# Small matmuls of a window scan: dt's weights zero-padded to 128 rows, B's transposes taken over all rows

## The chip, the cores and the metric

The kernel runs on one core of one Trainium2 chip. The metric is the time of one execution on the device in microseconds (us); the median of three executions is compared. The core has five engines that run side by side, each with its own order of instructions: TensorE (PE in the profile; PEld is its weight loads), VectorE (DVE), ScalarE (ACT), GpSimd (POOL) and SyncE (SP), which here only issues DMAs.

## The reference, cut to what matters

Layer 0 is a triangle attention over an image of 256 x 256 pixels with 128 channels; nothing in it is touched. Layer 1 is a window scan. After a depthwise convolution, windows of 8 x 8 pixels of the upper and the lower half of the image are put in a Hilbert order and merged to sequences of L = 128 tokens; two orders (rows first, columns first), each scanned forwards and backwards, make K = 4 scans with 256 channels and a state of 16.

```python
x_dbl = jnp.einsum('bkdl,kcd->bkcl', xs, x_proj_w)                # 8 + 16 + 16 rows per scan
dts, Bs, Cs = jnp.split(x_dbl, [DT_RANK, DT_RANK + D_STATE], axis=2)
dts = jnp.einsum('bkrl,kdr->bkdl', dts, dt_projs_w)                 # 8 rows -> 256 channels
dts = jax.nn.softplus(dts + dt_projs_b[None, :, :, None])
A = -jnp.exp(A_logs).reshape(K, D_INNER, D_STATE)
...
def step(h, inp):
    u, dt, Bl, Cl = inp
    dA = jnp.exp(dt[..., None] * A)
    h = h * dA + (dt * u)[..., None] * Bl[:, :, None, :]
    y = jnp.einsum('bkdn,bkn->bkd', h, Cl)
    return (h, y)
```

The results of the four scans are added, put back in image order, normalised, gated with silu(z) and projected to 128 channels.

## The kernel before, in words

*Bands, jobs, units.* Layer 1 is cut into 64 bands (8 rows by 64 columns in each image half). A band has 4 jobs: two groups of four sequences (`g`), each in two orders (`o`). A job has 32 units: 2 directions (`back`) x 4 quarters of the state (`q`) x 2 channel halves (`dh`) x 2 pairs of sequences (`p`). All is float32, for which a matmul that is no transpose shows as two MATMUL instructions in the trace.

*One unit.* ACT makes the decay exp(dt A) (`decay`, tile `da`, L1172). TensorE spreads dt u B over state and tokens (`input`, `b_p<-diag,dut`, L1185): the stationary operand is dt u with the tokens on 64 partitions, the moving one a block-diagonal copy of B (`diag`), loaded from DRAM. Matmuls on partitions 0 to 63 and 64 to 127 take turns. DVE scans (`scan`, `h<-da,b_p`, L1205). GpSimd multiplies a pair of units with C (`weigh`, `h<-h,cc`, L1212). TensorE adds the four states up while it transposes (`reduce`, `y_p<-ident,h`, L1223). `b_p` has two buffers, so the input of unit i waits for the scan of unit i - 2.

*One job's preparation.* `u_mm` gathers the tokens in scan order, `xd_mm` projects them (L949): all 128 rows of `wx`, of which rows 0 to 7 are dt's forward rank, 32 to 39 the backward one, 64 to 95 B and 96 to 127 C, the rest zero. `xd_ev` adds 1 to rows 8 and 40, so that the dt bias can be a weight row. Then come the two steps that are changed:
- `bt_mm` (L961) writes C to DRAM and transposes B's 32 rows of `xd`, four blocks of 128 tokens, to `bt_p`; `bt_ev` copies that to `bt`, and `spread` writes it to the block diagonals in DRAM, from which `diag_load` reads.
- `dt_mm` (L1015) multiplies 9 rows of `xd` (8 of the rank, one of ones) with the 9 rows of `wdt` at partition 0 or 32, by direction; it is called 4 times per job. `dt_act` and `dt_max` make softplus of it on ACT and DVE, `du_mul` dt u on GpSimd, `dut_mm` and `dut_ev` the transposed dt u.

*Order of the work.* Layer 1's order is written out by hand. The main loop runs over the units; `own_script` (for the job to come) and `script` (for the running one) say at which unit each preparation step is issued, with its cost in columns on TensorE. What belongs to the neighbouring bands is filler: `conv` (`cv_p`), `expand` (`in_p`), `finish` (`z_p`, `w_p`, `gated`), `store` (`o_p`, `res`). Filler with a cost is issued at odd units when there is credit for it: every unit adds `rate`, every scripted step takes its cost off.

```python
    rate, cap, slack = 350, 800, 128
...
            credit = min(credit + rate, cap)
            for cost, call in calls:
                credit -= cost
                call()
```

So a scripted step's cost decides when the filler behind it is issued. In the text, slot n of TensorE is what stands between the inputs of unit n and of unit n + 1.

*Memory.* `wts` holds weights and constants: `wdt` one tile of 2 x 256 columns, `perm` the two orders and `permt` their transposes. PSUM is full: 4 banks of `b_p`, 2 of `y_p`, one for the scripted steps (`side`: `u_p`, `xd_p`, `bt_p`, `dt_p`, `dut_p`), one for the filler (`fill`).

Of the kernel before, what the change touches and what calls it, by code (L numbers as in the profile page):

```python
# [12 lines left out]
F32 = mybir.dt.float32  # L13
# [6 lines left out]
P = 128  # L20
# [5 lines left out]
DI = 256  # L26
NS = 16
DTR = 8
# [8 lines left out]
NBLK = 4  # L37
# [30 lines left out]
def kernel(  # L68
# [28 lines left out]
    nc = tc.nc  # L97
# [88 lines left out]
                    in_=x_proj[dh * P : (dh + 1) * P, k, lo : lo + n],  # L186
                )

    wdt = wts.tile([P, 2, DI], F32, name="wdt")
    for back in range(2):  # L190
        at = 32 * back
        nc.scalar.dma_start(
            out=wdt[at : at + DTR], in_=dt_w[:, 2 * back : 2 * back + 2]
        )
        for o in range(2):
            for dh in range(2):
                j = 2 * (o + 2 * back) + dh
                nc.scalar.dma_start(
                    out=wdt[at + DTR : at + DTR + 1, o, dh * P : (dh + 1) * P],
                    in_=dt_b[:, j : j + 1].rearrange("p j -> j p"),  # L200
                )
    units_at = wts.tile([P, 1], F32, name="units_at")
# [13 lines left out]


    perm = wts.tile([P, 2, P], F32, name="perm")
    permt = wts.tile([P, 2, P], F32, name="permt")
    halves_of = ident.rearrange("p (y f x) -> p y f x", y=WIN, f=2)  # L220
    for o, positions in enumerate(hilbert_positions()):
        for s, (wy, wx_) in enumerate(positions):
# [1 line left out]
                perm[:, o, 2 * s : 2 * s + 2], halves_of[:, wy, :, wx_]  # L224
            )
    with tc.tile_pool(name="pmp", bufs=1, space=PSUM) as pp:
        pt_p = pp.tile([P, 2, P], F32, name="pt_p")
        for o in range(2):
            nc.tensor.transpose(pt_p[:, o], perm[:, o], ident)
        nc.vector.tensor_copy(permt, pt_p)  # L230

        ca_p = pp.tile([P, P], F32, name="ca_p")
        nc.tensor.matmul(ca_p, perm[:, 0], perm[:, 1], start=True, stop=True)
        carry = wts.tile([P, P], F32, name="carry")
        nc.vector.tensor_copy(carry, ca_p)
# [432 lines left out]
    class Band:  # L668
# [125 lines left out]
        def finish(self, g):  # L794

            if self.gated is None:
                self.gated = one_p.tile([P, 2, NSEQ, SEQ], F32, name="gated")
            for s2 in range(GS // 2):
                s = g * GS + 2 * s2
                yield 512  # L800
                z_p = fill("z_p")
                for dh in range(2):
                    nc.tensor.matmul(
                        z_p[:, dh * DI : (dh + 1) * DI],
                        win[:, DI + dh * P : DI + (dh + 1) * P],
                        self.xg[:, 1 : 1 + WIN, :, 1 + s * WIN : 1 + (s + 2) * WIN]
                        .rearrange("p y f x -> p (y f) x")
                        .rearrange("p y (s x) -> p s y x", s=2),
                        start=True,
                        stop=True,  # L810
                    )
                yield -2

                ysum = self.ysb[g, 1][:, 2 * s2 : 2 * s2 + 2]
                e = two_p.tile([P, 512], F32, name="e")
                nc.vector.tensor_scalar(e, z_p, FLOOR, None, ALU.max)
                st = two_p.tile([P, 2, 6], F32, name="st")
                mv = two_p.tile([P, 2, 2], F32, name="mv")
                for j in range(2):
                    nc.vector.bn_stats(st[:, j], ysum[:, j])  # L820
                for j in range(2):
                    nc.vector.bn_aggr(mv[:, j], st[:, j])
                yield 0
                logistic(e)
                rs = two_p.tile([P, 2], F32, name="rs")
                rsqrt(rs, mv[:, :, 1])
                neg = two_p.tile([P, 2], F32, name="neg")
                nc.scalar.activation(neg, rs, AF.Copy, scale=-1.0)
                nb = two_p.tile([P, 2], F32, name="nb")
                for j in range(2):  # L830
                    nc.scalar.activation(
                        nb[:, j : j + 1],
                        mv[:, j, 0:1],
                        AF.Identity,
                        scale=neg[:, j : j + 1],
                    )
                yield -2
                nc.vector.tensor_mul(e, e, z_p)
                yn = one_p.tile([P, 2, DI], F32, name="yn")
                for j in range(2):  # L840
                    nc.scalar.activation(
                        yn[:, j],
                        ysum[:, j],
                        AF.Identity,
                        bias=nb[:, j : j + 1],
                        scale=rs[:, j : j + 1],
                    )
                yield 256
                w_p = fill("w_p")
                for dh in range(2):  # L850
                    for j in range(2):
                        nc.tensor.transpose(
                            w_p[:, dh * DI + j * P : dh * DI + (j + 1) * P],
                            yn[:, j, dh * P : (dh + 1) * P],
                            permt[:, 1],
                        )
                yield 0
                for dh in range(2):
                    half = w_p[:, dh * DI : (dh + 1) * DI]
                    nc.scalar.activation(  # L860
                        half,
                        half,
                        AF.Identity,
                        bias=lb1[:, dh : dh + 1],
                        scale=lw1[:, dh : dh + 1],
                    )
                yield -2
                nc.vector.tensor_mul(
                    self.gated[:, :, s : s + 2].rearrange("p d s l -> p d (s l)"),
                    w_p.rearrange("p (d l) -> p d l", d=2),  # L870
                    e.rearrange("p (d l) -> p d l", d=2),
                )
# [26 lines left out]
    def token_blocks(t):  # L899

        return t.rearrange("c (h s t) -> c h s t", h=2, s=GS)
# [5 lines left out]
    class Job:  # L907
# [53 lines left out]
        def bt_mm(self):  # L961
            self.c_d = cdr.tile([2 * NS, GT], F32, name="c_d")
            for h in range(2):
                nc.sync.dma_start(
                    out=token_order(self.c_d)[:, h],
                    in_=token_blocks(self.xd[96:128])[:, h],
                )
            self.bt_p = side("bt_p")
            for i in range(NBLK):
                nc.tensor.transpose(  # L970
                    self.bt_p[:, i * 32 : (i + 1) * 32],
                    self.xd[64:96, i * P : (i + 1) * P],
                    ident[64:96, 64:96],
                )

        def bt_ev(self):
            self.bt = two_p.tile([P, NBLK, 2, NS], F32, name="bt")
            nc.scalar.copy(
                self.bt.rearrange("p b k n -> p (b k n)"), self.bt_p[:, 0 : NBLK * 32]
            )  # L980

        def spread(self):
# [31 lines left out]

        def dt_mm(self, back, dh):  # L1015
            self.dt_p = side("dt_p")
            rows = slice(32 * back, 32 * back + DTR + 1)
            nc.tensor.matmul(  # L1018
                token_order(self.dt_p),
                wdt[rows, self.o, dh * P : (dh + 1) * P],  # L1020
                token_blocks(self.xd[rows]),
                start=True,
                stop=True,
            )
# [93 lines left out]
        def own_script(self):  # L1118

            return {  # L1120
                7: [(256, lambda: self.u_mm(0))],
                8: [(0, lambda: self.u_ev(0))],
                9: [(256, lambda: self.u_mm(1))],
                10: [(0, lambda: self.u_ev(1))],
                15: [(512, lambda: self.xd_mm(0))],
                16: [(512, lambda: self.xd_mm(1))],
                17: [(0, lambda: self.xd_ev())],
                18: [(128, lambda: self.bt_mm())],
                19: [(0, lambda: self.bt_ev())],
                20: [(512, lambda: self.dt_mm(0, 0)), (0, lambda: self.spread())],  # L1130
                21: [(0, lambda: self.dt_act(0, 0))],
                22: [(0, lambda: self.dt_max(0, 0))],
                23: [(512, lambda: self.dt_mm(0, 1))],
                24: [(0, lambda: self.dt_act(0, 1)), (0, lambda: self.diag_load(0, 0))],
                26: [(0, lambda: self.dt_max(0, 1))],
                28: [(256, lambda: self.dut_mm(0, 0))],
                29: [(0, lambda: self.dut_ev(0, 0))],
                30: [(256, lambda: self.dut_mm(0, 1))],
                31: [(0, lambda: self.dut_ev(0, 1))],
            }  # L1140
# [301 lines left out]
```

## Time and profile before

| | us |
|---|---|
| median of three executions | 23599.31 |
| their range | 23597.42 to 23599.98 |
| the profiled execution | 23598.3 |
| its span, first to last instruction | 23596.4 |

| engine | busy us | share of the span |
|---|---|---|
| TensorE, matmuls | 22824.2 | 97% |
| TensorE, weight loads | 16986.3 | 72% |
| VectorE | 21652.4 | 92% |
| GpSimd | 21292.1 | 90% |
| ScalarE | 18542.0 | 79% |

Layer 0 takes about the first 2420 us, layer 1 the rest. In layer 1 every band after the first shows the same period, 330.2 us from its first scan to that of the next, so one band stands for all. A line of the profile names the engine, the source line, the tile written and those read. Matmuls are pipelined: [...] what a matmul costs is read from one start to the next. An engine's idle time is put down to what ended it.

### The profile page before, as it was taken

How to read it: one execution, taken by the hardware profiler on the slowest of the kernel's cores; microseconds unless marked ns; L12 is line 12 of the kernel's file. 1: busy time of each engine (PE TensorE's matmuls, PEld its weight loads, DVE VectorE, ACT ScalarE, POOL GpSimd, SP SyncE). 2: the span in 40 equal slices, each digit the busy share in tenths (PEclk: the TensorE clock that was granted, in tenths of full speed). 3: DMA queues.
4: the chain of work that ended last, by engine and by line, in shares of the span. 5: the costliest groups of instructions: out<-in, count | busy, mean ns of one | idle time of the engine just before them, and what ended most of it. 6: DMA issues, size and time to landing. Idle time of an engine off the chain costs nothing.

```text
span 23596.4 us, 427303 instructions
## 1 busy us (share of the span) xinstructions
PE 22824.2 (97%) x171020; PEld 16986.3 (72%) x171020; DVE 21652.4 (92%) x17940; ACT 18542.0 (79%) x35206; POOL 21292.1 (90%) x5966
## 2 busy tenths in 40 slices
PE   7999999999999999999999999999999999999999
PEld 2555677777777777777777777777777777777777
DVE  6888899999999999999999999999999999999998
ACT  5999777777777777777777777777777777777777
POOL 3777899999999999999999999999999999999999
PEclk9999999999999999999999999999999999999999
DMA  5222444444444444444444444444444444444444
GB/s 200 76 74 72 146 160 159 161 162 160 161 158 162 161 160 159 160 163 160 161 159 160 162 160 162 158 161 162 160 159 161 162 161 160 158 161 162 160 160 147
DMA packets 2000327, 3638.76 MB, mean 154 GB/s; under 512 B 1129584, under 2 KB 1131760, under 8 KB 1725824
## 3 DMA queue, kind: packets, MB, share of 16 engines
q1 hardware_dynamic: 1985616, 3602.35, 45.7%
q8 instruction: 1347, 22.07, 0.4%
q10 hardware_dynamic: 12720, 9.07, 0.1%
q14 instruction: 644, 5.28, 0.1%
HBM read 3467.33 MB, written 143.65 MB: 153 GB/s over the span
## 4 chain that ended last, share of the span: by engine, by line
PE 67%; DVE 16%; ACT 9%; issue 8%; DMA 0%; ACTq 0%; POOLq 0%; SPq 0%; POOL 0%; DVEq 0%
PE b_p L1185 23%; PE y_p L1223 21%; DVE h L1205 14%; PE dt_p L1018 4%; PE cv_p L769 4%; PE xd_p L949 2%; ACT da L1172 2%; PE aT_p L522 1%; PE dut_p L1052 1%; PE sc L465 1%; ACT w_p L860 1%; PE in_p L721 1%; PE o_p L885 1%; ACT e L132 1%; PE v_p L383 1%
## 5 line engine op out<-in xcount | busy, mean ns | idle before, releaser
L1212 POOL TENSOR_TENSOR h<-h,cc 128x2048 f32<-128x2048 f32 x4096 | 18598.0, 4551 | 1318.2 <-POOL h L1212 560.7
L1205 DVE TENSOR_TENSOR_SCAN h<-da,b_p 128x1024 f32<-128x1024 f32 x8192 | 18245.8, 2271 | 1212.6 <-PE b_p L1185 1193.2
L1172 ACT ACTIVATE da<-dt,am 128x508 f32<-128x508 f32 x16384 | 10396.5, 707 | 853.3 <-DVE h L1205 853.2
L1185 PE MATMUL b_p<-diag,dut 64*128 64x256 f32 x65536 | 8561.4, 395 | 430.0 <-DVE h L1205 365.7
L1223 PEld LDWEIGHTS y_p<-ident,h 128*128 128x128 f32 x65536 | 7130.2, 140 | 1408.4 <-issue 1296.3
L1223 PE MATMUL y_p<-ident,h 128*128 128x128 f32 x65536 | 8008.8, 276 | 25.1 <-issue 19.4
L1185 PEld LDWEIGHTS b_p<-diag,dut 64*128 64x128 f32 x65536 | 5851.7, 186 | 2916.9 <-issue 1331.2
L738 ACT ACTIVATE tap<-xin,wtap 128x512 f32<-128x512 f32 x2048 | 1504.2, 744 | 349.1 <-PE cv_p L769 349.0
L1041 POOL TENSOR_TENSOR du<-dt,u 128x512 f32<-128x512 f32 x1024 | 1309.1, 1278 | 57.9 <-DVE dt L1034 57.9
L769 PE MATMUL cv_p<-ident,tap 128*128 128x128 f32 x9216 | 1273.7, 275 | 5.1 <-DVE xct L788 3.8
L769 PEld LDWEIGHTS cv_p<-ident,tap 128*128 128x128 f32 x9216 | 1047.4, 141 | 232.4 <-issue 228.2
L1028 ACT ACTIVATE sp<-dt_p 128x512 f32<-128x512 f32 x1024 | 603.1, 589 | 777.5 <-PE dt_p L1018 777.5
L452 POOL TENSOR_TENSOR tm<-trib,mb 128x2048 f32<-128x2048 f32 x256 | 1167.1, 4559 | 10.7
L1018 PE MATMUL dt_p<-xd,wdt 9*128 9x512 f32 x2048 | 1149.8, 641 | 2.5 <-DVE dt L1034 2.2
L493 ACT ACTIVATE at<-at,nmax 128x256 f32<-128x256 f32 x2048 | 1019.5, 502 | 0.0
L1061 ACT COPY dut<-dut_p 128x512 f32<-128x512 f32 x1024 | 583.8, 570 | 292.9 <-PE dut_p L1052 292.9
L1163 ACT ACTIVATE da<-ident 128x16 f32<-128x16 f32 x1536 | 346.0, 225 | 549.2 <-DVE h L1205 547.4
L1029 ACT ACTIVATE sp<-sp,one 128x512 f32<-128x512 f32 x1024 | 743.1, 726 | 33.3
L729 ACT COPY xin<-in_p 128x440 f32<-128x440 f32 x384 | 201.7, 525 | 718.6 <-PE in_p L721 718.6
L478 DVE CUSTOM_DVE_ANT_0 at<-sc,tm 128x256 f32<-128x256 f32 x2048 | 738.1, 417 | 7.9 <-PE sc L465 7.4
L1034 DVE SCALAR_TENSOR_TENSOR dt<-sp,dt_p 128x512 f32<-128x512 f32 x1024 | 677.9, 662 | 13.9 <-ACT sp L1029 13.9
L1052 PE MATMUL dut_p<-ident,du 128*128 128x128 f32 x4096 | 650.2, 281 | 13.7 <-ACT dut L1061 8.7
(132 smaller groups left out, 15502.6 us busy)
## 6 DMA issues: line engine op xcount, KB each, us to landing
cc<-c_d SPq DMA_DIRECT2D x2048, 1024.0 KB
diag<-z SPq DMA_DIRECT2D x1024, 1024.0 KB
xt<-in_x_dram SPq DMA_DIRECT2D x16, 2048.0 KB
xt<-in_x_dram SPq DMA_DIRECT2D x32, 1024.0 KB
xn_d<-xn SPq DMA_DIRECT2D x32, 1024.0 KB
xn<-xn_d SPq DMA_DIRECT2D x128, 256.0 KB
mb<-in_mask_dram SPq DMA_DIRECT2D x128, 256.0 KB
xr<-in_x_dram SPq DMA_DIRECT2D x128, 256.0 KB
```

The source lines that it names most:

```text
L452: nc.gpsimd.tensor_add(self.tm, trib.rearrange("p h m n -> p (h m) n"), self.pair.mb[:, self.row].unsqueeze(1).to_broadcast([P, 2 * NH, IMG]),
L493: nc.scalar.activation(self.at[hp][:, j, :], self.at[hp][:, j, :], AF.Exp, bias=self.nmax[hp][:, j : j + 1], scale=-1.0, accum_out=self.de ...
L738: nc.scalar.activation(scaled.rearrange("p s (y x) -> p s y x", x=WIN), self.xin[:, dh] .rearrange("p y f x -> p (y f) x")[:, 2 * dy : 2 * ...
L769: nc.tensor.matmul(cv_p[:, s], now[:, s], ident, start=(tap == 0 and s == 0), stop=(tap == 8 and s == GS - 1), is_transpose=True, skip_gro ...
L1018: nc.tensor.matmul(token_order(self.dt_p), wdt[rows, self.o, dh * P : (dh + 1) * P], token_blocks(self.xd[rows]), start=True, stop=True,)
L1041: nc.gpsimd.tensor_mul(token_blocks(du), token_order(self.dt[back][dh]), token_blocks(self.u[:, dh]),)
L1052: nc.tensor.transpose(self.dut_p[:, h * DI + dh * P : h * DI + (dh + 1) * P], self.du[back][dh][:, (2 * h + p) * P : (2 * h + p + 1) * P], ...
L1172: nc.scalar.activation(da[:, :, j, lo:hi], dt[:, :, lo:hi], AF.Exp, scale=am[:, a0 : a0 + 1])
L1185: nc.tensor.matmul(b_p[:, s, :, h * 64 : (h + 1) * 64].rearrange("p n t -> p t n"), job.dut[self.back][rows, p, h, self.dh * P : (self.dh ...
L1205: nc.vector.tensor_tensor_scan(out=out_, data0=d0, data1=d1, initial=0.0, op0=ALU.mult, op1=ALU.add)
L1212: nc.gpsimd.tensor_mul(self.pair, self.pair, cc.rearrange("p n s t -> p s n t"))
L1223: nc.tensor.matmul(job.y_p[:, 2 * p + s, self.dh * P : (self.dh + 1) * P], self.h[:, s, j], ident, start=(first and s == 0 and j == 0), st ...
```

## The change

`wdt` gets a tile of 128 rows for each direction, filled with zeros before the 9 rows of weights and bias are loaded; `dt_mm` multiplies all 128 rows of `xd`. `bt_mm` transposes all 128 rows of `xd`, so `bt_p` has 4 x 128 columns instead of 4 x 32, and `bt_ev` picks columns 64 to 95 of each block. The cost entered for `bt_mm` goes from 128 to 256. `bt` has one buffer instead of two, and of `permt` only the half that is read is kept. The other costs in the scripts stay.

```diff
-    wdt = wts.tile([P, 2, DI], F32, name="wdt")
+    wdt = wts.tile([P, 2, 2, DI], F32, name="wdt")
+    nc.vector.memset(wdt, 0.0)
     for back in range(2):
         at = 32 * back
         nc.scalar.dma_start(
-            out=wdt[at : at + DTR], in_=dt_w[:, 2 * back : 2 * back + 2]
+            out=wdt[at : at + DTR, back], in_=dt_w[:, 2 * back : 2 * back + 2]
         )
...
-                    out=wdt[at + DTR : at + DTR + 1, o, dh * P : (dh + 1) * P],
+                    out=wdt[at + DTR : at + DTR + 1, back, o, dh * P : (dh + 1) * P],
...
-    permt = wts.tile([P, 2, P], F32, name="permt")
+    permt = wts.tile([P, P], F32, name="permt")
...
-        pt_p = pp.tile([P, 2, P], F32, name="pt_p")
-        for o in range(2):
-            nc.tensor.transpose(pt_p[:, o], perm[:, o], ident)
+        pt_p = pp.tile([P, P], F32, name="pt_p")
+        nc.tensor.transpose(pt_p, perm[:, 1], ident)
...
-                            permt[:, 1],
+                            permt,
...
                 nc.tensor.transpose(
-                    self.bt_p[:, i * 32 : (i + 1) * 32],
-                    self.xd[64:96, i * P : (i + 1) * P],
-                    ident[64:96, 64:96],
+                    self.bt_p[:, i * P : (i + 1) * P],
+                    self.xd[:, i * P : (i + 1) * P],
+                    ident,
                 )
...
-            self.bt = two_p.tile([P, NBLK, 2, NS], F32, name="bt")
+            self.bt = two_p.tile([P, NBLK, 2, NS], F32, name="bt", bufs=1)
             nc.scalar.copy(
-                self.bt.rearrange("p b k n -> p (b k n)"), self.bt_p[:, 0 : NBLK * 32]
+                self.bt.rearrange("p b k n -> p b (k n)"),
+                self.bt_p.rearrange("p (b r) -> p b r", b=NBLK)[:, :, 64:96],
             )
...
-            rows = slice(32 * back, 32 * back + DTR + 1)
             nc.tensor.matmul(
                 token_order(self.dt_p),
-                wdt[rows, self.o, dh * P : (dh + 1) * P],
-                token_blocks(self.xd[rows]),
+                wdt[:, back, self.o, dh * P : (dh + 1) * P],
+                token_blocks(self.xd),
                 start=True,
                 stop=True,
             )
...
-                18: [(128, lambda: self.bt_mm())],
+                18: [(256, lambda: self.bt_mm())],
```

## The prediction

> **What bounds the kernel now.** I read the chain of the page first, then the stage table, the table of waits, and TensorE's timeline over one band.
>
> ```profile
> PE 67%; DVE 16%; ACT 9%; issue 8%; DMA 0%; ACTq 0%; POOLq 0%; SPq 0%; POOL 0%; DVEq 0%
> PE b_p L1185 23%; PE y_p L1223 21%; DVE h L1205 14%; PE dt_p L1018 4%; PE cv_p L769 4%; PE xd_p L949 2%; ACT da L1172 2%; PE aT_p L522 1%; PE dut_p L1052 1%; PE sc L465 1%; ACT w_p L860 1%; PE in_p L721 1%; PE o_p L885 1%; ACT e L132 1%; PE v_p L383 1%
> ```
>
> TensorE holds two thirds of the chain, and dt_p alone 4% of it, nearly all that it takes in total (1024 calls at 1.05 us or more are 4.6% of the span): most dt matmuls stand where TensorE decides. But the stage table, here for about one band of layer 1, shows three engines close together (busy: PE, PEld, DVE, ACT, POOL):
>
> ```profile
> 12000.00:12330.00 330.00, 322.53 (x2429) 246.61 (x2428) 308.66 (x183) 259.18 (x461) 309.36 (x81) 1.00 0.48 160
> ```
>
> ```profile
> DVE h L1205 <- PE b_p L1185: 1193.2, 1792, 1.8
> PEld b_p L1185 <- DVE h L1205: 997.9, 1807, 1.9
> ```
>
> Scans wait for TensorE and TensorE waits for scans, each about a thousand us in all: the lead changes hands within a band. So a gain on TensorE counts in some stretches and not in others. In TensorE's timeline the first column is the start of a group of instructions:
>
> ```profile
> 12017.72 1.12 PE L1018 MATMUL dt_p<-xd,wdt 9*128 9x512 f32 x2
> 12018.77 1.97 PE L1223 MATMUL y_p<-ident,h 128*128 128x128 f32 x16
> 12020.58 0.60 PE L769 MATMUL cv_p<-ident,tap 128*128 128x128 f32 x4
> 12021.11 2.00 PE L1185 MATMUL b_p<-diag,dut 64*128 64x256 f32 x16
> 12023.03 1.97 PE L1223 MATMUL y_p<-ident,h 128*128 128x128 f32 x16
> 12024.93 1.12 PE L1018 MATMUL dt_p<-xd,wdt 9*128 9x512 f32 x2
> 12025.98 0.66 PE L769 MATMUL cv_p<-ident,tap 128*128 128x128 f32 x4
> 12026.57 2.00 PE L1185 MATMUL b_p<-diag,dut 64*128 64x256 f32 x16
> ```
>
> ```profile
> 12055.31 1.02 PE L949 MATMUL xd_p<-u,wx 128*128 128x512 f32 x2
> 12056.26 1.14 PE L1185 MATMUL b_p<-diag,dut 64*128 64x256 f32 x8
> 12057.95 1.14 PE L1185 MATMUL b_p<-diag,dut 64*128 64x256 f32 x8 [0.56 <-DVE h L1205]
> 12059.02 1.13 PE L949 MATMUL xd_p<-u,wx 128*128 128x512 f32 x2
> 12059.98 1.91 PE L1223 MATMUL y_p<-ident,h 128*128 128x128 f32 x16
> 12061.73 0.60 PE L852 MATMUL w_p<-permt,yn 128*128 128x128 f32 x4
> 12062.26 2.00 PE L1185 MATMUL b_p<-diag,dut 64*128 64x256 f32 x16
> 12064.18 0.43 PE L970 MATMUL bt_p<-ident,xd 32*128 32x32 f32 x4
> 12064.55 1.97 PE L1223 MATMUL y_p<-ident,h 128*128 128x128 f32 x16
> 12066.35 0.60 PE L1081 MATMUL y_p<-ident,skip 128*128 128x128 f32 x4
> ```
>
> The reader is to compare starts. xd_p streams the same 512 columns as dt_p, but with all 128 rows: it is what dt_p becomes.
>
> **The change, part by part.**
> *dt matmul after y_p.* From y_p to b_p with dt_p and cv_p between: 26.57 - 23.03 = 3.54 us; with cv_p alone (18.77 to 21.11) 2.34. The 9-row dt_p costs 1.20. xd_p after y_p starts without a delay and hands over to b_p after 0.95, of which 0.09 is the change to 64 rows that every group before b_p pays (cv_p to b_p 0.53, four transposes at 0.109 being 0.44): 0.86. Saved: 0.34. Where b_p follows dt_p at once, that 0.09 was owed anyway: dt_p costs 1.05 there, and 0.19 is saved.
> *dt matmul after b_p.* dt_p to y_p 1.05, y_p to the next 1.81: 2.86. xd_p to y_p 0.96, y_p to the next 1.75: 2.71. Saved: 0.15.
> Per band (16 dt matmuls): 8 after b_p, 6 after y_p before 128-row work, 2 after y_p before b_p: 8 x 0.15 + 6 x 0.34 + 2 x 0.19 = 3.6 us.
> A rule speaks against this. The Trainium skill (TensorE: Matmul & The Clock Gate, "Why this matters for your kernels") says that a single matmul of 32 rows takes the same time as one of 128, tiling paying only by concurrency; by it dt_p saves nothing. But TensorEngine Tiling ("Key Properties") says that a change of tiling mode drains TensorE, and the rows put a price on it: 0.09 to 0.1 us at each end of dt_p, and a weight load that the next group no longer hides. I take the rows; the rule goes to a rival.
> *B's transposes.* bt_p to y_p is 0.37 now. Four transposes of 128 columns cost 0.44. Loss 0.07 each, 4 per band: 0.3 us. The first one's weight load after b_p is exposed in both, on bt_p or on y_p.
> TensorE therefore gets 3.6 - 0.3 = 3.3 us per band; over 64 bands about 215 us of work gone.
> *bt's evacuation* reads 128 columns with gaps in place of 128 together, on ACT (0.25 us, not late for anything but the z writes). I take 0; it copies as many elements, so no gain; the other bound, an estimate of 0.1 us more for each of 256, is 25 us of ACT, covered by ACT's idle time (259 of 330 us busy). With one bt buffer it waits for z writes issued a job (some 82 us) earlier: 0, unless SP runs a job behind, which no wait shows.
> *Once:* a memset of 1024 columns on DVE and wdt's ten DMAs on ACT's queue behind it, at 30 us, while layer 0 still loads x; one transpose less: 0 (bounds 0 and +1.5 us, the work itself). The DMAs stay ten, and no queue gets more of them.
> *What moves.* bt_mm is entered at 256 instead of 128, so the filler gets 128 less credit per job. The instruction order in the built program shows 12 changed slots in each band, the same in all four bands that I compared: in three places four cv_p transposes (0.44 us) go from a dt slot (units 4, 86, 118) one or two slots on; z_p, its DVE work and w_p of the second finish go from units 20 and 24 to 22 and 26; three o_p matmuls go from units 28, 30, 32 to 30, 32, 34. On SP the store of res falls behind a diag load and one cc load, on POOL the memset of xg behind one h multiply; both are loaded for work many slots later: 0, and if cc were late a scan's weighing would wait, up to 1 us per band.
>
> **What reaches the end.** Band from 12013.8 us, 330.2 long. Between TensorE's idle moments it leads; there savings count, up to the waits of the scans:
> - 0 to 33 us: waits 0.93, 0.27, 0.99, 0.56; dt saves 0.15 + 0.34. The moved cv_p finds cover. -0.49.
> - 33 to 77: DVE leads. dt savings are lost. But this stretch holds a wait that the move touches:
>
> ```profile
> 12080.61 0.69 DVE L868 TENSOR_TENSOR gated<-w_p,e 128x512 f32<-128x512 f32 x1 [0.69 <-ACT w_p L860]
> ```
>
>   w_p came behind a dt matmul there; at unit 26 none is ahead of it, and a dt evacuation fills DVE before it. I take -0.5, between 0 and -0.69.
> - 77 to 111: TensorE leads (waits 0.10, 0.35, 0.66, 0.33). dt saves 0.15 + 0.19, but o_p (0.86) now stands here: +0.5. With the line above: 0 together.
> - 111 to 157: dt 0.15 + 0.34, bt -0.07, against a last wait of 0.34: -0.26.
> - 157 to 202: waits 1.13 and 1.0: -0.49. GpSimd, busy without a gap from 140 to 180 us, then waits 0.76 for the scan and can just follow.
> - 202 to 243: 0.49 - 0.07, and cv_p moved behind the long wait of 0.99, where DVE's dt evacuation covers part of it: -0.6 (at least -0.42).
> - 243 to 286: DVE leads: 0.
> - 286 to 330: -0.42.
> Sum -2.26 to -2.35, say -2.33 us per band, x 64 = -149. The profiled execution took 23598.3 us (span 23596.4), 1 us below the median of 23599.3, so: 23450.
>
> **The rivals.**
> *All of it counts:* 3.3 us per band, if DVE and GpSimd follow wherever TensorE gets faster: 23384. For: both have over 20 us of slack per band. Against: no dt matmul at 33 to 77 and 243 to 286 has a scan waiting behind it.
> *Absorbed:* DVE (308.7 of 330) and GpSimd (309.4) take the lead at once, and new waits replace the old: 0 to -0.6 us per band, 23560 to 23600. Against: waits of 0.99 to 1.13 us right behind dt_p.
> *Slower:* the rule holds, the row count does not matter and the excess of dt_p comes from its strided output, which stays. Then only the price is paid: o_p at 77 to 111 without dt's relief, 0.86, and 3 x 0.07 for bt in the leading stretches: +1.07 us per band, +68: 23668. It decides as soon as a dt matmul of the leading stretches (12 per band) saves less than 0.09 us. Against: xd_p hands over to y_p in 0.96, dt_p in 1.05, with the same columns. That the change doesn't do what it says is this case too.
>
> **How the numbers follow.** Partial gain 0.64, all of it 0.17, absorbed 0.12, slower 0.07. About 0.2% (47 us) can be told from no change. Partial gain's own range is 23390 to 23520 (the unknowns at 33 to 111 us are worth -0.2 to +0.5 per band, at 202 to 243 0.2, the SP queue 1). The range reaches from all of it to the edge of absorbed: 23375 to 23565. Faster 0.83 (all of the first two, a little of the third), same 0.10, slower 0.07.
>
> **What would show it.** Right: dt_p 128 rows wide, 0.96 from dt_p to y_p and 0.86 from dt_p to cv_p between starts; bt_p to y_p about 0.49, its first exposed weight load included; the band at about 327.9 us; the wait of DVE's gated near 12080 gone; fewer waits of h for b_p. Wrong: dt_p still 1.05 between starts, TensorE's idle time before b_p grown by some 200 us with the band at 330, or h waiting longer for b_p around o_p at 77 to 111 us.

## The result, and the profile after

The changed kernel takes 23460.2 us (median of six runs, 23457.96 to 23461.18), against 23598.8 for the kernel before on the same chip: ratio 0.9941, interval 0.9928 to 0.9954, or 138.6 us less. The prediction said 23450. The profiled execution took 23461.2 us, its span is 23459.3. Line numbers in the profile after are one higher than before from the weights to `dt_mm` and past it.

TensorE's timeline, the same places as before (the band starts at 11950.8 us here, at 12013.8 before; first column the start of a group):

```profile
11954.64 1.12 PE L1019 MATMUL dt_p<-xd,wdt 128*128 128x512 f32 x2
11955.60 1.91 PE L1224 MATMUL y_p<-ident,h 128*128 128x128 f32 x16
11957.34 0.60 PE L770 MATMUL cv_p<-ident,tap 128*128 128x128 f32 x4
11957.87 2.00 PE L1186 MATMUL b_p<-diag,dut 64*128 64x256 f32 x16
11959.80 1.96 PE L1224 MATMUL y_p<-ident,h 128*128 128x128 f32 x16
11961.60 1.02 PE L1019 MATMUL dt_p<-xd,wdt 128*128 128x512 f32 x2
11962.56 2.15 PE L1186 MATMUL b_p<-diag,dut 64*128 64x256 f32 x16
```

Compare starts again. dt_p to y_p is 0.96 us (1.05 before), y_p to the next 1.74 (1.81). After y_p, dt_p starts without the delay (y_p to dt_p 1.80; 1.90 before) and hands over to b_p after 0.96, where 1.05 stood. The cv_p group that followed dt_p is gone from this slot. The last row is 2.15 long where 2.00 is usual: within these 16 matmuls TensorE now waits a little for a scan. The profile does not name so short a wait, but in the trace the ninth matmul starts 0.05 us after a scan has ended, the same as where a scan is named.

B's transposes, with the rows around them:

```profile
11998.69 2.00 PE L1186 MATMUL b_p<-diag,dut 64*128 64x256 f32 x16
12000.62 0.66 PE L971 MATMUL bt_p<-ident,xd 128*128 128x128 f32 x4
12001.12 1.91 PE L1224 MATMUL y_p<-ident,h 128*128 128x128 f32 x16
12002.86 0.60 PE L1082 MATMUL y_p<-ident,skip 128*128 128x128 f32 x4
```

bt_p to y_p 0.50 (0.37 before), y_p to the next 1.74 (1.80): 0.07 more in all. bt's evacuation with gaps takes ScalarE 251 ns (median; 248 before), so taking it for nothing was right.

The second finish of the band, on DVE:

```profile
12020.81 0.66 DVE L1035 SCALAR_TENSOR_TENSOR dt<-sp,dt_p 128x512 f32<-128x512 f32 x1
12021.39 0.68 DVE L869 TENSOR_TENSOR gated<-w_p,e 128x512 f32<-128x512 f32 x1
12021.99 8.81 DVE L1206 TENSOR_TENSOR_SCAN h<-da,b_p 128x1024 f32<-128x1024 f32 x4
12031.94 4.46 DVE L1206 TENSOR_TENSOR_SCAN h<-da,b_p 128x1024 f32<-128x1024 f32 x2 [1.14 <-PE b_p L1186]
```

`gated` starts right behind dt's evacuation: its wait of 0.69 us is gone. Ten us later a scan waits 1.14 for TensorE, where 0.35 stood; there the moved o_p shows.

The chain, the stage table and the waits:

```profile
PE 65%; DVE 19%; issue 9%; ACT 7%; DMA 0%; ACTq 0%; POOL 0%; POOLq 0%; DVEq 0%; SPq 0%
PE b_p L1186 22%; PE y_p L1224 21%; DVE h L1206 15%; PE cv_p L770 4%; PE dt_p L1019 4%; PE xd_p L950 2%; PE aT_p L523 1%; PE dut_p L1053 1%; ACT da L1173 1%; PE sc L466 1%; ACT w_p L861 1%; PE in_p L722 1%; DVE gated L869 1%; PE o_p L886 1%; DVE dt L1035 1%
```

```profile
12000.00:12330.00 330.00, 321.61 (x2448) 249.34 (x2445) 310.92 (x184) 261.45 (x464) 311.42 (x81) 1.00 0.48 162
```

```profile
PEld b_p L1186 <- DVE h L1206: 1068.9, 1811, 2.5
DVE h L1206 <- PE b_p L1186: 1050.1, 1597, 1.6
```

Of 330 us TensorE is now busy 321.6 (322.5 before), DVE 310.9 (308.7) and GpSimd 311.4 (309.4), so the two do more work in the same time and stand closer to TensorE. DVE's share of the chain went from 16 to 19%, TensorE's from 67 to 65%. Scans wait 143 us less for TensorE (1193.2 before), about what the kernel gained; TensorE's loads wait 71 us more for scans (997.9 before). Part of TensorE's time gain became idle time of TensorE.

### The profile page after: what moved, and what is told of

Read it like the earlier page. It is cut to its first block, busy times and chain, and to the rows that moved or that the text cites. A ratio compares the mean times of both kernels' runs of the same rounds, so it can differ in the third digit from the quotient of the medians.

```text
span 23459.3 us, 427688 instructions
## 1 busy us (share of the span) xinstructions
PE 22625.5 (96%) x171019; PEld 17048.5 (73%) x171019; DVE 21657.5 (92%) x17941; ACT 18544.5 (79%) x35206; POOL 21298.7 (91%) x5966
## 4 chain that ended last, share of the span: by engine, by line
PE 65%; DVE 19%; issue 9%; ACT 7%; DMA 0%; ACTq 0%; POOL 0%; POOLq 0%; DVEq 0%; SPq 0%
PE b_p L1186 22%; PE y_p L1224 21%; DVE h L1206 15%; PE cv_p L770 4%; PE dt_p L1019 4%; PE xd_p L950 2%; PE aT_p L523 1%; PE dut_p L1053 1%; ACT da L1173 1%; PE sc L466 1%; ACT w_p L861 1%; PE in_p L722 1%; DVE gated L869 1%; PE o_p L886 1%; DVE dt L1035 1%
## 5 line engine op out<-in xcount | busy, mean ns | idle before, releaser
L1029 ACT ACTIVATE sp<-dt_p 128x512 f32<-128x512 f32 x1024 | 602.9, 589 | 788.4 <-PE dt_p L1019 788.4
L1019 PE MATMUL dt_p<-xd,wdt 128*128 128x512 f32 x2048 | 1102.5, 620 | 2.5 <-DVE dt L1035 2.2
```

The costliest lines, as they stand in the source:

```text
L1019: nc.tensor.matmul(token_order(self.dt_p), wdt[:, back, self.o, dh * P : (dh + 1) * P], token_blocks(self.xd), start=True, stop=True,)
```

## The experiments

"Shift" below is how much earlier or later a scan starts within its band than in the kernel before, as the mean over bands 20 to 59, earlier being negative; the band is 330.21 us before and 328.01 in the changed kernel.

**Wide dt alone.** The changed kernel with bt's old transposes and their old cost.

```diff
-                    self.bt_p[:, i * P : (i + 1) * P],
-                    self.xd[:, i * P : (i + 1) * P],
-                    ident,
+                    self.bt_p[:, i * 32 : (i + 1) * 32],
+                    self.xd[64:96, i * P : (i + 1) * P],
+                    ident[64:96, 64:96],
...
-                18: [(256, lambda: self.bt_mm())],
+                18: [(128, lambda: self.bt_mm())],
```

> dt_p with all 128 rows, bt_mm and its cost of 128 as before, so the filler stands as before. Theory (the row tile costs dt_p 0.15 us after b_p, 0.34 after y_p, 0.19 between y_p and b_p, and this counts where TensorE leads): -0.49, 0, -0.33, -0.33, -0.49, -0.49, 0, -0.49 us over the eight stretches of a band, -2.6 in all, x 64 = -168: 23431 us, band 327.6. Rival 'the moved filler brought it' (rows do not matter): 23598, band 330.2. Rival 'all TensorE time counts': 3.6 per band, 23369.

Measured: 23456.4 us (before 23600.0; 0.994, interval 0.9925 to 0.9955), band 327.95. The wide dt matmul alone brings all that the change brings, 144 us. That refutes the rival that the moved filler did it, and the one that all TensorE time counts (23369). The price after y_p, before 128-row work, is what was read off xd_p, 0.86 us from dt_p to cv_p (1.05 before):

```profile
11958.02 1.97 PE L1223 MATMUL y_p<-ident,h 128*128 128x128 f32 x16
11959.82 1.02 PE L1018 MATMUL dt_p<-xd,wdt 128*128 128x512 f32 x2
11960.68 0.60 PE L770 MATMUL cv_p<-ident,tap 128*128 128x128 f32 x4
```

The kernel is 25 us slower than my own sum. Nearly all of that lies in two stretches: at 77 to 111 us of the band the shift is -0.11 where I expected -0.33, at 111 to 157 it is -0.23 instead of -0.33. In both, TensorE comes early and then waits for a scan inside a group of b_p. The group behind the second dt_p near 95 us of the band, before and with the wide dt alone:

```profile
12109.81 2.04 PE L1185 MATMUL b_p<-diag,dut 64*128 64x256 f32 x16
```

```profile
12044.25 2.26 PE L1185 MATMUL b_p<-diag,dut 64*128 64x256 f32 x16
```

**Wide B alone**, the other half: 9 rows for dt, the transposes over all rows, entered at 256.

```diff
-                    self.bt_p[:, i * 32 : (i + 1) * 32],
-                    self.xd[64:96, i * P : (i + 1) * P],
-                    ident[64:96, 64:96],
+                    self.bt_p[:, i * P : (i + 1) * P],
+                    self.xd[:, i * P : (i + 1) * P],
+                    ident,
...
-                18: [(128, lambda: self.bt_mm())],
+                18: [(256, lambda: self.bt_mm())],
```

> dt_p with 9 rows as before; only the transposes over all 128 rows, entered at 256. Theory: DVE's gated wait near 80 us of the band goes (-0.63), o_p at 77 to 111 us costs 0.86 again, bt +0.08 in three leading stretches: +0.23 + 0.24 = +0.47 us per band, +30: 23628 us. Rival 'the moved filler brought it': most of the gain is here, below 23500. Rival 'all TensorE time counts': +0.3 per band, 23618.

Measured: 23596.7 (0.9998, interval 0.999 to 1.0007), band 330.13. Neither the loss of 30 us nor a gain: the interval holds no change. The transposes cost what I expected, 0.23 us per band against the moved filler alone (band 329.90, below); the moved filler is what I had wrong: it gains 0.31 where I expected a loss of 0.23.

**Wide dt only where DVE leads**, four of a band's sixteen dt matmuls. This kernel and those with other row counts below start from the wide dt alone (bt's old transposes and cost); `rows` then indexes both `wdt` and `xd`.

```diff
+            rows = slice(0, P) if self.o == 1 and self.g == back else slice(32 * back, 32 * back + DTR + 1)
```

> As dt_only, but 128 rows only for the four dt matmuls of a band that stand where DVE leads (slots 22, 24, 98 and 100); the other twelve keep their 9 rows. Theory: TensorE gets 2 x (0.15 + 0.34) = 0.98 us per band free there and idles longer; band 330.2, 23598 us (at most 20 less). Rival 'all TensorE time counts': -0.98 x 64 = -63, 23536 us.

Measured: 23599.4 (1.0, interval 0.9991 to 1.0009), band 330.23. Nothing comes of it, as the theory has it; "all TensorE time counts" asked for 63 us. The wide matmuls are there; the timeline of this kernel shows where their time goes:

```profile
12068.23 1.12 PE L1019 MATMUL dt_p<-xd,wdt 128*128 128x512 f32 x2
12069.19 1.91 PE L1224 MATMUL y_p<-ident,h 128*128 128x128 f32 x16
12071.03 1.14 PE L1186 MATMUL b_p<-diag,dut 64*128 64x256 f32 x8
12072.87 1.13 PE L1186 MATMUL b_p<-diag,dut 64*128 64x256 f32 x8 [0.70 <-DVE h L1206]
12073.93 1.97 PE L1224 MATMUL y_p<-ident,h 128*128 128x128 f32 x16
12075.74 1.02 PE L1019 MATMUL dt_p<-xd,wdt 128*128 128x512 f32 x2
12076.84 0.33 PE L853 MATMUL w_p<-permt,yn 128*128 128x128 f32 x1
12077.34 0.55 PE L853 MATMUL w_p<-permt,yn 128*128 128x128 f32 x3 [0.16 <-ACT yn L842]
```

The same place before has dt_p to y_p 1.05, then

```profile
12074.43 1.13 PE L1185 MATMUL b_p<-diag,dut 64*128 64x256 f32 x8 [0.56 <-DVE h L1205]
12075.49 1.97 PE L1223 MATMUL y_p<-ident,h 128*128 128x128 f32 x16
12077.39 1.12 PE L1018 MATMUL dt_p<-xd,wdt 9*128 9x512 f32 x2
12078.44 0.99 PE L852 MATMUL w_p<-permt,yn 128*128 128x128 f32 x4
```

The first matmul's 0.15 us is in b_p's longer wait for the scan (0.56 to 0.70). The second's is in w_p, which comes sooner and waits for ScalarE's yn: dt_p to the first w_p is 1.10 instead of the 0.86 that an unhindered successor has.

**The moved filler alone**: the kernel before, with nothing but the cost.

```diff
-                18: [(128, lambda: self.bt_mm())],
+                18: [(256, lambda: self.bt_mm())],
```

> The kernel before with bt_mm's cost entered as 256 and nothing else: the filler moves as in the change, no TensorE work changes. Theory: -0.63 for the gated wait, +0.86 for o_p at 77 to 111 us, the three moved cv_p groups find cover: +0.23 us per band, +15: 23613 us. Rival 'the moved filler brought it': below 23500. Rival 'all TensorE time counts': 23598.

Measured: 23580.9 (0.9992, interval 0.9984 to 1.0001), band 329.90: the interval just reaches no change, but the band is 0.31 us shorter on the mean of 40, and 64 x 0.31 are the 20 us. My theory said 0.23 longer. Shift by stretch: -0.36 by 33 us; then -0.48 by 82 and +0.86 after it, as expected, so +0.02 at 97; -0.25 at 202 to 243; -0.08 at 286 to 330. The miss is in the first stretch and at 202 to 243, where I had let the moved cv_p pass for nothing. TensorE's timeline of this kernel:

```profile
12019.53 1.96 PE L1223 MATMUL y_p<-ident,h 128*128 128x128 f32 x16
12021.42 1.12 PE L1018 MATMUL dt_p<-xd,wdt 9*128 9x512 f32 x2
12022.48 2.00 PE L1185 MATMUL b_p<-diag,dut 64*128 64x256 f32 x16
12024.40 1.97 PE L1223 MATMUL y_p<-ident,h 128*128 128x128 f32 x16
12026.21 0.60 PE L1081 MATMUL y_p<-ident,skip 128*128 128x128 f32 x4
12026.65 1.04 PE L769 MATMUL cv_p<-ident,tap 128*128 128x128 f32 x8
12027.61 2.00 PE L1185 MATMUL b_p<-diag,dut 64*128 64x256 f32 x16
```

With cv_p away, the 9-row dt_p stands directly before b_p. There it costs 1.05 and not 1.20 (y_p to b_p is 22.48 - 19.53 = 2.95, against 3.54 with a cv_p of 0.44 in it): one change of the tile's height is owed to b_p anyway. So moving a neighbour saved 0.15 of dt_p's price, a gain that the wide dt_p no longer has to give. And b_p takes 2.00 in the last row, where the group at that place before took 2.14: a wait of TensorE for a scan that hid inside a group. These two are 0.29 of the 0.36; 0.07 came from the band's start. At 202 to 243 us dt_p keeps its neighbours, y_p and cv_p, and the 0.25 is such waits alone: two b_p groups took 2.14 and 2.25 before, 2.00 and 2.14 here.

**32 rows**: a whole row tile for each direction, 23 of its rows zero.

```diff
+            rows = slice(32 * back, 32 * back + 32)
```

> As dt_only, but each dt matmul takes the 32 rows of its own row tile (9 of weights, 23 of zeros) instead of 128. Theory (the row tile makes the price, not the number of rows): no gain, 23599 us, band 330.2, dt_p to y_p still 1.05 us between starts. Rival (an odd number of 9 rows is what is slow): as dt_only, 23456.

Measured: 23598.7 (1.0, interval 0.999 to 1.0009), band 330.22.

```profile
12016.56 1.12 PE L1019 MATMUL dt_p<-xd,wdt 32*128 32x512 f32 x2
12017.61 1.97 PE L1224 MATMUL y_p<-ident,h 128*128 128x128 f32 x16
```

Still 1.05 from dt_p to y_p. Rows of zeros are not what helps.

**64 rows**, the height that b_p has.

```diff
+            rows = slice(0, 64)
```

> As dt_only, but 64 rows, 0 to 63, the tile shape that b_p has. Theory (a price at each change of the tile's height): after b_p the change moves from before dt_p to behind it, so one change less, and the weight load can run ahead: dt_p costs 0.85 instead of 1.05 us there, 8 per band, 6 of them where TensorE leads; after y_p as before (1.20 before cv_p). -1.2 to -1.3 us per band, x 64: 23517 us. Rival (all of the gain comes from having all 128 rows): 23599.

Measured: 23499.8 (0.9958, interval 0.9943 to 0.9973), band 328.68. Two thirds of the gain come with 64 rows, so it is not the full array as such.

```profile
11970.67 2.00 PE L1186 MATMUL b_p<-diag,dut 64*128 64x256 f32 x16
11972.50 1.02 PE L1019 MATMUL dt_p<-xd,wdt 64*128 64x512 f32 x2
11973.45 1.97 PE L1224 MATMUL y_p<-ident,h 128*128 128x128 f32 x16
11975.25 0.60 PE L770 MATMUL cv_p<-ident,tap 128*128 128x128 f32 x4
11975.78 2.00 PE L1186 MATMUL b_p<-diag,dut 64*128 64x256 f32 x16
11977.71 1.96 PE L1224 MATMUL y_p<-ident,h 128*128 128x128 f32 x16
11979.60 1.12 PE L1019 MATMUL dt_p<-xd,wdt 64*128 64x512 f32 x2
11980.65 0.66 PE L770 MATMUL cv_p<-ident,tap 128*128 128x128 f32 x4
```

After b_p, of equal height, dt_p starts 1.83 us after b_p did instead of 1.93, and hands over in 0.95; the change comes only then, so y_p takes 1.80. The two gaps sum up to 0.2 saved. After y_p nothing is saved: 1.05 to cv_p. The price goes with the change of height. (In the two places after y_p where b_p comes next, dt_p and b_p, of one height, start 0.01 us apart and run side by side. What that is worth stays open: the scan is waited for either way, and one y_p to the next takes 4.96 us here and 4.95 with the wide dt alone.) It came 17 us better than my sum, and that in a place that I had not counted: both stretches where DVE leads became 0.2 us shorter each. There dt_p after b_p ends 0.2 us sooner, which with 128 rows it does not: they save the change behind dt_p, not the one ahead of it. ScalarE's chain to w_p starts behind that dt_p: from dt's softplus to yn, which w_p needs, ScalarE has no gap over 0.04 us in the trace. DVE's `gated` waits for its end: in all `gated` waits 137.2 us in this kernel, 161.4 before and 162.5 with the wide dt alone.

```profile
ACT sp L1029 <- PE dt_p L1019: 703.2, 386, 2.9
DVE gated L869 <- ACT w_p L861: 137.2, 256, 3.6
```

Before, and with the wide dt alone:

```profile
DVE gated L868 <- ACT w_p L860: 161.4, 256, 3.6
DVE gated L869 <- ACT w_p L861: 162.5, 256, 3.6
```

ScalarE's wait for dt_p, 703.2 here, is 777.5 before and 788.4 in the changed kernel: the change lets ScalarE wait no less.

**The change without the moved filler**: bt_mm entered at 128.

```diff
-                18: [(256, lambda: self.bt_mm())],
+                18: [(128, lambda: self.bt_mm())],
```

> The change with bt_mm entered at 128, so the filler stands as before, with the 128-row transposes. Theory: dt_only (-2.26 us per band) and 0.08 more for bt in three leading stretches: -2.02, 23470 us. Rival (the moved filler costs, as the prediction had it at 77 to 111 us, and its gains elsewhere do not make up for it): below 23460, better than the change.

Measured: 23472.0 (0.9946, interval 0.9931 to 0.9961), band 328.25. As expected, and the rival is out: the moved filler is worth 0.24 us per band to the change.

**The change without bt's wide transposes**, but with the cost of 256.

```diff
-                    self.bt_p[:, i * P : (i + 1) * P],
-                    self.xd[:, i * P : (i + 1) * P],
-                    ident,
+                    self.bt_p[:, i * 32 : (i + 1) * 32],
+                    self.xd[64:96, i * P : (i + 1) * P],
+                    ident[64:96, 64:96],
```

> The change with bt's old transposes of 32 rows, but entered at 256: the wide dt matmul and the moved filler without bt's 0.08. Theory (what dt and the moved filler bring overlaps, since both end at the same waits): the change less 0.08 in two or three leading stretches, -2.35 to -2.45 us per band, 23446 us. Rival (they add up, -2.26 and -0.31): 23435.

Measured: 23445.1 (0.9934, interval 0.9918 to 0.9951), band 327.79. What dt and the moved filler bring does not add up (-2.26 and -0.31 would be 327.64). Against the changed kernel this is 15 us better: bt's wide transposes are a loss in it of 0.22 us per band.

**Height by the neighbour**: 64 rows for dh = 0, which follows b_p, 128 for dh = 1, which follows y_p; bt as before the change.

```diff
+            rows = slice(0, P // 2) if dh == 0 else slice(0, P)
```

> As dt_only, but by its neighbour each dt matmul takes the height that was cheapest: 64 rows for dh = 0, which follows b_p, 128 rows for dh = 1, which follows y_p. Theory (price at each change of the tile's height; in rows64 dt_p after b_p also ended 0.2 us sooner for ScalarE, which shortened the two stretches where DVE leads): dt_only's -2.26 us per band, 0.05 more in five leading stretches, 0.2 more in each of the two DVE stretches: -2.9, 23414 us. Rival (in those stretches rows64 only gained something that dt_only has already): -2.3 to -2.5, 23445.

Measured: 23413.6 (0.9921, interval 0.9904 to 0.9937), band 327.34: the theory's number, and better than both kernels, 188 us below the kernel before in the same comparison (23601.3); the changed kernel was 139 below in its own.

**The same with the moved filler.**

> As mix, with bt_mm entered at 256, so that the filler moves (bt's transposes as before, 32 rows). Theory: dt_move's -2.42 us per band, 0.05 more in five leading stretches and 0.2 more in the second DVE stretch (in the first the moved w_p has no wait left): -2.87, 23416 us, the same as mix within 10. Rival (moved filler and mixed rows add up): -2.9 - 0.3, 23395.

Measured: 23417.9 (0.9923, interval 0.9908 to 0.9937), band 327.37: the same as without it, as expected. With the mixed heights the moved filler brings nothing more.

## Why the prediction was right

The shift gained in each stretch (us), predicted, and measured in the changed kernel and with the wide dt alone:

| stretch of the band, us | predicted | changed kernel | wide dt alone |
|---|---|---|---|
| 0 to 33 | -0.49 | -0.54 | -0.48 |
| 33 to 111 | 0 | -0.10 | -0.11 |
| 111 to 157 | -0.26 | -0.15 | -0.23 |
| 157 to 202 | -0.49 | -0.48 | -0.48 |
| 202 to 243 | -0.6 | -0.56 | -0.49 |
| 243 to 286 | 0 | 0.00 | 0.00 |
| 286 to 330 | -0.42 | -0.37 | -0.48 |
| band | -2.33 | -2.20 | -2.26 |

The predicted stretches add up to -2.26 us, which is 23455; the 0.07 more in the -2.33 behind 23450 has no stretch of its own. Single stretches are off by up to 0.11 us, some too high and some too low, and the misses nearly cancel. The mechanism came out as told; that the total is only 10 us off is in part luck.

- *The price of dt_p's tile* was read off xd_p, and the runs show it to the hundredth: dt_p to y_p 0.96 us, dt_p to cv_p 0.86. The rule of the Trainium skill that a matmul of 32 rows takes as long as one of 128 (TensorE: Matmul & The Clock Gate, "Why this matters for your kernels") holds for the columns streamed: behind b_p, the two matmuls of a dt_p start 0.53 us apart with 9, with 32 and with 128 rows. It does not hold for what a matmul costs among its neighbours: 32 rows gave nothing, 64 gave it on one side, and 128 on the other. The output of dt_p is strided as before, so the rival that put the price there is out. A change of tiling mode drains TensorE, says the Trainium skill (TensorEngine Tiling, "Key Properties"). The traces agree in that each change of height costs about 0.1 us (y_p to dt_p 1.90 against 1.80); the draining itself they don't show. Beside it stands a weight load that is no longer hidden: behind a change it starts together with its matmul instead of 0.11 us ahead, and the next matmul starts 0.06 (transposes) to 0.1 us (dt_p: 0.53 against 0.43) later.
- *That it counts only where TensorE leads* was shown by the wide dt in the four trailing places (0 us) beside the wide dt everywhere (144 us). It holds for the 128-row tile; dt_p of 64 rows is the exception, told above.
- *The gated wait and o_p* went as said: -0.63 by 82 us of the band (-0.5 predicted), +0.53 after it (+0.5). The two nearly cancel.
- *111 to 157 was sized too high.* The second dt matmul there stands before b_p, which is worth 0.19 and not 0.34; the prediction's own count of two such places per band had it, its sum by stretch did not. With the wide dt alone there is no bt loss, and still only 0.23 came: b_p's group behind the first dt_p takes 2.10 instead of 2.00, so 0.1 went to waiting for a scan. It is 0.23 again with 64 rows and with the mixed heights, where the two dt matmuls save other amounts: the scan sets it.
- *The moved cv_p* was given cover at 0 to 33 us, worth nothing, and about 0.18 at 202 to 243. Alone it gains 0.36 and 0.25 there, 0.15 of it by putting dt_p beside b_p in the first stretch. In the change, where that 0.15 is gone, it is worth 0.06 and 0.15, and the moved filler as a whole 0.24.
- *bt* cost 0.07 on TensorE as read, and in the change three leading stretches of it as predicted: 0.22 us (the change without bt's wide transposes, beside the change). With the filler in its old place it costs 0.30 (the wide dt alone, beside the change without the moved filler): there it counts also at 33 to 77, where DVE leads. The scan at 67 us shifts by -0.40 with bt wide and by -0.48 without.

## What to carry to other kernels

Cost a matmul by the starts of its neighbours with and without it, not by its own duration: here a tenth of a us lay in each change of row-tile height, and the cure was to give each small matmul the height of what stands before it, at no cost in streamed columns. Before counting a saving, find in one period who leads in which stretch; a tie between three engines at 93 to 98% turned 3.3 us of TensorE work per band into 2.2. When a change carries a second edit for symmetry, try the halves: B's wide transposes cost 0.22 us per band here and gave nothing back.

## What the runs showed that I had not expected

A dt matmul beside b_p is 0.15 us cheaper than the same one among 128-row work, so a pure reordering of filler (20 us faster in the median, its interval touching no change) gained in part through the tile's height (0.15 us of a band's 0.31); the rest went into waits of TensorE that hid inside its groups. And where DVE leads, a TensorE saving can still count if ScalarE's chain to a DVE wait begins behind that matmul: ending 0.2 us sooner, dt_p with 64 rows shortened each of those stretches by 0.2 us.
